# Order of the first loads, the root of block 0 and the grouping of LoRA products in a gated FFN kernel with an S4 convolution

## The chip, the cores and the metric

One core of a Trainium2 chip runs the kernel. The metric is the time of one execution on the device, in microseconds (us); the median of several runs counts. A profile is one execution recorded by the hardware; its times start with the span of that execution. PE is the matrix engine (PEld its weight loads), DVE the vector engine, ACT the scalar engine, POOL the GpSimd engine, SP the engine that issues most transfers.

## The reference, cut to what matters

The input x has 2 x 1024 tokens of 512 features, all in float32.

```python
xn = _layernorm(x, axis=-1)                       # mean and variance over the 512 features, eps 1e-5
s = _L0_attn_ref(xn, ...)                         # one S4 kernel K of 512 taps, causal convolution along the features, plus D*xn
def _lora_linear(x, w, a, b):                     # rank R = 16, SCALING = 2
    base = jnp.einsum('bsd,od->bso', x, w)
    low = jnp.einsum('bsr,or->bso', jnp.einsum('bsd,rd->bsr', x, a), b)
    return base + low * SCALING
h1 = _lora_linear(xn, w1, lora_A1, lora_B1)       # 512 -> 1376
h3 = _lora_linear(xn, w3, lora_A3, lora_B3)
g = _silu(_lora_linear(jax.nn.silu(h1) * h3, w2, lora_A2, lora_B2))   # 1376 -> 512
out = x + s * g
```

## The kernel before, in words

**Tiling.** The 2048 tokens are four blocks of 512 (`TB`), each of four tiles of 128 tokens (`NTT`). Two blocks form a super block (`sb`). A tile is normalized with tokens on the partitions, transposed on PE against an identity (L304) and copied by ACT out of PSUM (L312, L314, L315), so that features stand on the partitions. The 1376 hidden units are ten chunks of 128, taken in five pairs, and a last chunk of 96.

**Products by seven.** Each product of two 2x2 arrangements of blocks is made from seven block products instead of eight (Strassen's scheme in Winograd's form). For this DVE makes sums of token blocks (`outer_token_sum` L328, `inner_token_sum` L341 to L347) and of weight blocks (`outer_weight_sums` L441, `inner_weight_sum` L453), POOL those of the last chunk (L492 to L495). A `Chain` does the seven products on PE (L756), snapshots of PSUM on ACT (L776, L794), and totals on DVE (L780, L870). Pair 0 and the last chunk start with the outer scheme alone, since blocks 2 and 3 arrive later.

**LoRA** is merged into the weights: PE multiplies the two factors (`lora_product` L383, contraction over 16 rows) and DVE adds twice the result to the weights (`merge` L393). A set of factors lies at 32 * group of the partitions, 16 rows of it, and up to four groups can work at once in different row groups of PE. `lora_last` (L475) does the last chunk with groups 0 (w1) and 1 (w3); `merge_pair` (L408) does half of pair 0 with the same two groups, one half at a time; `merge_whole_pair` (L419) does a whole pair with four groups, whose groups 2 and 3 hold a second copy of the same factors.

**The opening.** `load_x` (L225) issues block 0's four tiles in turn on SP and ACT (L231). Then come the factors of groups 0 and 1, one set on SP and one on ACT (L372, L373), then on SP block 1 (four tiles), the last chunk's weights (L470), pair 0's weights (four transfers, L402), blocks 2 and 3, pair 1, and the second copy of the factors. Eight completion semaphores are used in turn, so that the ninth transfer and each one after it waits for the one eight places earlier. On ACT a one-element Silu (L973) brings the activation table in early. Keep-warm products of the identity (L991) fill PE at the start.

DVE makes mean and variance of each tile (`norm_stats`, L247 and L248) and the reciprocal root for the whole block (`norm_root`, L278: L281, then eight operations of `rsqrt` L57 to L66, then the shift L284). ACT and POOL normalize two tiles each (L293, L297).

**What sets the order.** The order on PE, DVE, ACT and POOL is the program's own: `manual_schedule` keeps what the program writes. In the opening (L965 to L1018) that is the written order; from there on an event list, `at(place, what)` and `after(delay, what)`, is popped by place (L1254). A place orders work and is no time: an instruction runs when its engine reaches it and its data are there. On PE the written order of the opening is: 18 keep-warm products, `lora_last` (8 products), 4 keep-warm products, the transposes of block 0, the first step of the last chunk, half of pair 0's LoRA (4 products), the next step, the transposes of block 1, the first step of pair 0, the other half of LoRA (4 products), and then products on token sums.

Of the kernel before, what the change touches and what calls it, by code (L numbers as in the profile page):

```python
# [12 lines left out]
F32 = mybir.dt.float32  # L13
# [4 lines left out]
P = 128  # L18
# [3 lines left out]
HID = 1376  # L22
# [27 lines left out]
def rsqrt(nc, pool, v, shape):  # L50


    y = pool.tile(shape, F32, tag="rs_y", name="rs_y")
    t = pool.tile(shape, F32, tag="rs_t", name="rs_t")
    part = 3.0 / 8.0
    c2 = part * 0.703952253
    nc.vector.tensor_scalar(  # L57
        y.bitcast(I32), v.bitcast(I32), -0.5, float(0x5F1FFFF9), ALU.mult, ALU.add
    )
    nc.vector.tensor_tensor(t, y, y, ALU.mult)  # L60
    nc.vector.scalar_tensor_tensor(t, t, -c2, v, ALU.mult, ALU.mult)
# [46 lines left out]
def s4_gated_ffn(  # L108
# [101 lines left out]
    def value(tag="s"):  # L210
        return upool.tile([P, TB], F32, tag=tag, name=tag, bufs={"s": 10, "c": 4}[tag])
# [11 lines left out]


    def load_x(b):  # L225
        room = (None, None, t_in[4], t_in[6])[b]
        tiles = []
        for tt in range(NTT):
            t = value() if room is None else room[:, tt, :]
            queue = nc.scalar if b == 0 and tt % 2 else nc.sync  # L230
            queue.dma_start(out=t, in_=x[bass.ds(b * TB + tt * P, P), :])  # L231
            tiles.append(t)
        return tiles

    norms, sums_of_x = {}, {}

# [38 lines left out]
            norms[b][:, :, 1], sums_of_x[b][:, 2, :], 1.0 / DIM, None, mult  # L275
        )

    def norm_root(mv, *blocks):  # L278
        n = len(blocks) * NTT
        veps = small.tile([P, n], F32, tag="veps", name="veps")  # L280
        nc.vector.tensor_scalar(veps, mv[:, :, 1], EPS, None, add)  # L281
        rstd = rsqrt(nc, small, veps, [P, n])
# [16 lines left out]
    def transpose(b, tiles, tag="aux"):  # L299
        sb, low = divmod(b, 2)  # L300
        for tt in tiles:
            ps = bank(tag)
            for dc in range(NDC):
                nc.tensor.transpose(  # L304
                    ps[:, dc * P : (dc + 1) * P],
                    x_in[b][tt][:, dc * P : (dc + 1) * P],
                    ident,
                )
            at_ = slice(tt * P, (tt + 1) * P)
            halves = ps.rearrange("p (c k t) -> p c k t", c=2, k=2)  # L310
            if low == 0:
                nc.scalar.copy(xr[:, 0:2, sb, :, at_], halves)  # L312
# [68 lines left out]
    def lora_product(ps, group, dc, lo, n, start=True):  # L381
        d, h = lora_factors(group, lo, n)
        nc.tensor.matmul(  # L383
            ps,
            lhsT=d[:, dc * P : (dc + 1) * P],
            rhs=h,
            start=start,
            stop=True,
            skip_group_check=True,
        )  # L390
# [14 lines left out]
                )  # L405
        return w

    def merge_pair(c, w, half, tag="aux"):  # L408

        ps = [bank(tag), bank(tag)]  # L410
        for k in range(2):
            for v in range(2):
                n = slice(k * 2 * P, (k + 1) * 2 * P)
                lora_product(ps[v][:, n], v, 2 * half + k, PAIR_AT[c], 2 * P, k == 0)
        for v in range(2):
            to = w[:, (1, 2, 0, 3)[2 * v + half]].rearrange("p k m h -> p (k m h)")
            after(1.6 + v, lambda to=to, v=v: merge(to, ps[v]))
# [45 lines left out]
    def load_last():  # L463
        both = const.tile([P, 2, 2 * NDC * LASTR], F32, tag="w2b", name="last")
        w, s = (
            both[:, i].rearrange("p (a b h) -> p a b h", a=n, h=LASTR)
            for i, n in enumerate((2, 4))
        )
        for v, src in enumerate((w1T, w3T)):
            nc.sync.dma_start(  # L470
                out=w[:, v], in_=src[:, LAST * P :].rearrange("(dc p) h -> p dc h", p=P)
            )
        return w, s

    def lora_last():  # L475
        ps = [bank("y"), bank("y")]
# [485 lines left out]
        for i, p in places:  # L962
            at(7 * n + p, lambda i=i: step(i))

    x_in = {0: load_x(0)}  # L965
    warm = const.tile([P, 1], F32, name="warm")
    nc.gpsimd.memset(warm, 0.0)
# [5 lines left out]
    nc.scalar.activation(warm, warm, AF.Silu)  # L973
    x_in[1] = load_x(1)
    make_upper_triangular(nc, tri, 1.0, diag=True)
    w_last, s_last = load_last()
    w_pair, s_pair = {0: load_pair(0)}, {c: {} for c in range(NPAIR)}
    x_in[2], x_in[3] = load_x(2), load_x(3)
    w_pair[1] = load_pair(1)
    for v, f in enumerate(factors):  # L980
        load_lora(nc.sync, 2 + v, *f, LSPLIT, HID)

    def other_factors():
        for v, (_, h) in enumerate(factors):
# [18 lines left out]
    ps_last = lora_last()  # L1003
    mv = norm_tile(0)
    norm_stats(0, range(NTT))
    norm_root(mv, 0)
    normalize(0)

    keep_warm(primed[1], 4)
    transpose(0, range(NTT))  # L1010
    mv = norm_tile(1)
    norm_stats(1, range(2))
    merge_last(w_last, ps_last, 0)
    norm_stats(1, range(2, NTT))
    norm_root(mv, 1)
    merge_last(w_last, ps_last, 1)
    mv_late = norm_tile(2, 3)
    ab_last = last_operands(w_last, s_last)  # L1018

# [37 lines left out]
            add_chain(2 + 7 * c + n, pair_chain(c, n), places)  # L1057
    at(-10, lambda: normalize(1))
    at(-9.9, lambda: last_sums(w_last, s_last))
    at(-9, lambda: merge_pair(0, w_pair[0], 0))  # L1060
    at(-3.8, lambda: merge_pair(0, w_pair[0], 1))
    for i in range(2):
        at(-6 + i, lambda i=i: transpose(1, range(2 * i, 2 * i + 2), "y"))
    for n, name in enumerate((3, 2, 1)):
        at((-2.3, -1.5, -0.45)[n], lambda name=name: outer_token_sum(0, name))
        at(-0.6 + 0.3 * n, lambda name=name: outer_weight_sums(w_pair[0], (name,)))
    at(0.4, lambda: outer_token_sum(0, 4))
    at(0.8, lambda: outer_weight_sums(w_pair[0], (4,)))
    for tt in range(NTT):
        at(-6 + 0.8 * tt, lambda tt=tt: norm_stats(2, (tt,)))  # L1070
        at(-1.4 + 0.1 * tt, lambda tt=tt: act_sums(3, tt))
        at((-0.3, -0.2, 1.7, 1.8)[tt], lambda tt=tt: act_squares(3, tt))
    at(-0.9, lambda: act_means(3))
    at(1.9, lambda: act_variances(3))
    at(6.9, lambda: norm_root(mv_late, 2, 3))
    at(7.3, lambda: normalize(2))
    at(7.7, lambda: normalize(3, (0,)))
    for n, place in enumerate((12.1, 12.8, 13.7, 14.4)):
        b, i = divmod(n, 2)
        at(place, lambda b=b, i=i: transpose(2 + b, range(2 * i, 2 * i + 2)))  # L1080
# [514 lines left out]
```

## Time and profile before

| what | value |
|---|---|
| runs | 442.51, 442.54, 442.62 us; median 442.54 |
| profiled execution | 442.84 us, of which the span is 441.0 us |
| busy in the span | PE 434.3 us (98%), DVE 317.6 (72%), POOL 207.9 (47%), ACT 144.3 (33%) |
| granted clock of PE | 0.998 of full speed, mean |
| transfers | 53.61 MB, mean 122 GB/s |
| first statistics on DVE | 3.98 us |
| `lora_last` on PE | from 7.89 us |
| first transposes of block 0 and of block 1 on PE | 11.01 and 18.11 us |
| first token sum (L328) on DVE | 21.55 us |

A row of the timeline is: start, length, engine, line, operation, written tile <- read tiles, shapes, count, and in brackets the idle time of that engine before it and what ended it. Rows of one kind that follow each other are put together, and a matmul in float32 is two records. A row of a table by stretch gives busy time (and count) of PE, PEld, DVE, ACT and POOL, then PE's granted clock, the share of the DMA engines that are busy, and GB/s. A row of a transfer gives the issuing queue, the count, the size and the median time from issue to landing.

### The profile page before, as it was taken

What the parts mean: (1) busy time and instruction counts of PE and PEld (TensorE: products, weight loads), DVE (VectorE), ACT (ScalarE), POOL (GpSimd) and SP (SyncE); (2) the same over time, 40 slices, a digit from 0 to 9 for tenths busy, and PEclk for the clock granted to TensorE, in tenths of its full rate; (3) what the DMA queues carried; (4) which work ended last, traced back from release to release, by engine and by line L of the source; (5) the groups of instructions that cost most, each with busy time, mean ns of one, the idle gap of its engine ahead of it and who ended that gap; (6) DMA issues with size and microseconds to landing.
All of it is one profiled execution on the core that took longest, in us unless ns stands there. A gap on an engine that the chain in (4) does not pass through costs nothing.

```text
span 441.0 us, 5158 instructions
## 1 busy us (share of the span) xinstructions
PE 434.3 (98%) x1704; PEld 269.1 (61%) x1704; DVE 317.6 (72%) x536; ACT 144.3 (33%) x296; POOL 207.9 (47%) x156
## 2 busy tenths in 40 slices
PE   7999999999999999999999999999999999999996
PEld 7645334344444444444443446888898999999996
DVE  5899999954974687469745796979786885653234
ACT  2777242453255324532453242211101212212221
POOL 1416468895689368946894468400000122222221
PEclk9999999999999999999999999999999999999999
DMA  8931304025102500250035526395901832422211
GB/s 242 364 83 44 124 0 149 10 84 159 36 24 80 159 24 25 88 170 25 25 129 206 162 94 214 94 364 189 344 33 71 296 129 95 144 97 95 77 67 48
DMA packets 35467, 53.61 MB, mean 122 GB/s; under 512 B 4689, under 2 KB 21521, under 8 KB 35313
## 3 DMA queue, kind: packets, MB, share of 16 engines
q1 hardware_dynamic: 35088, 52.69, 36.3%
q10 hardware_dynamic: 352, 0.60, 0.4%
q8 instruction: 13, 0.21, 0.2%
q14 instruction: 14, 0.11, 0.1%
HBM read 33.88 MB, written 19.40 MB: 121 GB/s over the span
## 4 chain that ended last, share of the span: by engine, by line
PE 86%; DVE 7%; DMA 2%; ACT 2%; issue 1%; POOL 0%; SPq 0%; DVEq 0%; ACTq 0%; POOLq 0%
PE x L756 43%; PE y L756 22%; PE w L756 11%; PE aux L930 4%; PE w L930 2%; DMA s<-in_x_dram 1%; DVE xt L328 1%; DVE s L453 1%; DVE w L441 1%; DMA w<-in_w1T_dram 1%; PE y L529 1%; PE aux L711 1%; DVE t_in L343 1%; ACT c L254 1%; DVE aux L1310 1%
## 5 line engine op out<-in xcount | busy, mean ns | idle before, releaser
L1313 POOL TENSOR_TENSOR o<-o,xin 128x512 f32<-128x512 f32 (+1 forms) x17 | 23.3, 1369 | 133.0 <-DVE o L1312 133.0
L837 POOL TENSOR_TENSOR s<-c,s 128x512 f32<-128x512 f32 (+1 forms) x44 | 63.2, 1442 | 17.6 <-ACT c L829 12.4
L776 ACT COPY s<-x 128x512 f32<-128x512 f32 (+1 forms) x54 | 31.5, 584 | 84.5 <-PE x L756 84.4
L756 PE MATMUL x<-t_in,s 128*128 128x512 f32 (+1 forms) x148 | 55.4, 501 | 0.0
L870 POOL TENSOR_TENSOR s<-ua_three,s 128x512 f32<-128x512 f32 x20 | 35.9, 1793 | 25.4 <-DVE s L780 25.4
L780 DVE TENSOR_TENSOR s<-s,y 128x512 f32<-128x512 f32 (+1 forms) x54 | 36.0, 679 | 15.7 <-PE y L756 10.6
L756 PEld LDWEIGHTS x<-t_in,s 128*128 128x128 f32 x148 | 26.6, 190 | 23.3 <-issue 11.7
L870 POOL TENSOR_TENSOR ua_three<-ua_three,s 128x512 f32<-128x512 f32 x20 | 30.6, 1529 | 13.8 <-DVE s L780 13.8
L756 PE MATMUL y<-t_in,s 128*128 128x256 f32 (+1 forms) x108 | 35.9, 459 | 0.1
L1335 ACT COPY z<-x 128x256 f32<-128x256 f32 x24 | 8.8, 371 | 70.5 <-PE x L756 70.4
L870 POOL TENSOR_TENSOR s<-u_three,s 128x512 f32<-128x512 f32 x20 | 29.4, 1474 | 1.8 <-ACT c L829 1.0
L1310 DVE TENSOR_TENSOR aux<-aux,m 128x384 f32<-128x384 f32 x32 | 18.1, 565 | 15.8 <-PE aux L930 14.3
L829 ACT ACTIVATE c<-c 128x512 f32<-128x512 f32 x40 | 25.2, 632 | 12.9 <-DVE c L870 12.9
L756 PEld LDWEIGHTS y<-t_in,s 128*128 128x128 f32 x108 | 20.1, 190 | 11.6 <-issue 8.1
L794 ACT COPY w<-x 128x512 f32<-128x512 f32 (+1 forms) x37 | 21.1, 570 | 11.6 <-PE x L756 11.5
L870 POOL TENSOR_TENSOR u_three<-ua_three,u_three 128x512 f32<-128x512 f32 x10 | 15.6, 1556 | 13.4 <-DVE u_three L780 13.3
L756 PE MATMUL x<-t_in,w 128*128 128x512 f32 x40 | 21.0, 605 | 0.0
L756 PE MATMUL x<-xt,w 128*128 128x512 f32 x40 | 20.7, 598 | 0.0
L756 PE MATMUL x<-xr,w 128*128 128x512 f32 x40 | 20.6, 614 | 0.0
L756 PE MATMUL x<-xr,s 128*128 128x512 f32 x40 | 20.5, 614 | 0.0
L756 PE MATMUL x<-xt,s 128*128 128x512 f32 x40 | 20.4, 592 | 0.0
L756 PE MATMUL y<-xt,w 128*128 128x512 f32 x40 | 19.8, 592 | 0.0
(302 smaller groups left out, 908.7 us busy)
## 6 DMA issues: line engine op xcount, KB each, us to landing
g_dram<-s SPq DMA_DIRECT2D x40, 256.0 KB, 2.1
g<-g_dram SPq DMA_DIRECT2D x10, 512.0 KB, 5.8
xin<-in_x_dram SPq DMA_DIRECT2D x16, 256.0 KB, 2.7
out_dram<-o SPq DMA_DIRECT2D x14, 256.0 KB, 2.0
t_in<-g_dram SPq DMA_DIRECT2D x6, 512.0 KB, 4.1
w<-in_w1T_dram SPq DMA_DIRECT2D x10, 256.0 KB, 3.6
w<-in_w3T_dram SPq DMA_DIRECT2D x10, 256.0 KB, 4.9
t_in<-in_x_dram SPq DMA_DIRECT2D x8, 256.0 KB, 5.7
```

Of the source, the lines that this page charges most:

```text
L254: nc.scalar.activation(value("c"), x_in[b][tt], AF.Copy, accum_out=sums_of_x[b][:, 0, tt : tt + 1])
L756: nc.tensor.matmul(ps[:, cols], lhsT=lhsT, rhs=rhs if parts == 1 else rhs[:, cols], start=first and i == 0 and part == 0, stop=i == len(pa ...
L776: nc.scalar.copy(t, self.x)
L780: nc.vector.tensor_tensor(t, t, self.y, add)
L794: nc.scalar.copy(self.w, self.x)
L829: nc.scalar.activation(c, c if src is None else src, AF.Silu)
L837: nc.gpsimd.tensor_tensor(g, act, g, mult)
L870: (nc.vector if o < 20 else nc.gpsimd).tensor_tensor(to, a, b, add)
L930: nc.tensor.matmul(to[:, n * P : (n + 1) * P], lhsT=x_, rhs=by, start=start, stop=True, skip_group_check=True,)
L1310: nc.vector.tensor_tensor(y[:, P:], y[:, P:], m[:, n * P : (n + 3) * P], add)
L1313: (nc.vector if last else nc.gpsimd).tensor_tensor(o, o, self.xin[h][:, cols], add)
L1335: nc.scalar.copy(t, xb)
```

## The change

Four things change together.

- **Loads.** Block 1 is two transfers of 512 KB, one on SP and one on ACT, issued right behind block 0's tiles and into the room of `t_in[7]`. The factors of groups 0 and 1 follow, then on SP the last chunk's weights, the second copy of the factors (groups 2 and 3, formerly last), pair 0, blocks 2 and 3 (two transfers each instead of four), pair 1.
- **Root.** Block 0's root is a Sqrt on ACT, a reciprocal on DVE and one Newton step on DVE. The early table load is that of Sqrt; a one-element Silu behind the copies of block 0's transposes brings the other table in. The other blocks keep `rsqrt`.
- **LoRA of pair 0** is done by `merge_whole_pair` with four groups in one pass, ahead of block 1's transposes; `merge_pair` is gone. On DVE its four merges follow each other behind block 1's root.
- **Places.** Three keep-warm products instead of four ahead of block 0's transposes, whose third tile uses a bank of tag x; block 1's first tile borrows a bank of x; merging of the last chunk's w3 goes ahead of block 1's root; three of block 2's four tiles of statistics go from between the merges and the first token sums to behind the weight sums (places -5.2, -4.4, -3.6 to 0.84, 0.85, 0.9); normalization of block 2 goes from 7.3 to 7.7.

On ACT the silu of the last chunk (`c<-w`, L829) now comes behind all copies of block 1 instead of between them.

```diff
     def load_x(b):
...
+        if b == 0:
+            tiles = [value() for _ in range(NTT)]
+            for tt, t in enumerate(tiles):
+                (nc.sync, nc.scalar)[tt % 2].dma_start(out=t, in_=x[bass.ds(tt * P, P), :])
+            return tiles
+        room = (None, t_in[7], t_in[4], t_in[6])[b]
+        for tt in range(0, NTT, 2):
+            queue = nc.scalar if b == 1 and tt else nc.sync
+            queue.dma_start(
+                out=room[:, tt : tt + 2, :],
+                in_=x[bass.ds(b * TB + tt * P, 2 * P), :].rearrange("(n p) d -> p n d", p=P),
+            )
+        return [room[:, tt, :] for tt in range(NTT)]
...
+    def refined(mv, veps):
+
+        shape = list(veps.shape)
+        y = small.tile(shape, F32, tag="rs_y", name="rs_y")
+        t = small.tile(shape, F32, tag="rs_t", name="rs_t")
+        root = small.tile(shape, F32, tag="root", name="root", bufs=1)
+        nc.scalar.activation(root, mv[:, :, 1], AF.Sqrt, bias=eps)
+        nc.vector.tensor_scalar(veps, mv[:, :, 1], EPS, None, add)
+        nc.vector.reciprocal(y, root)
+        nc.vector.tensor_tensor(t, y, y, mult)
+        nc.vector.scalar_tensor_tensor(t, t, -0.5, veps, mult, mult)
+        nc.vector.scalar_tensor_tensor(y, t, 1.5, y, add, mult)
+        return y
...
-    x_in = {0: load_x(0)}
+    x_in = {0: load_x(0), 1: load_x(1)}
...
-    nc.scalar.activation(warm, warm, AF.Silu)
-    x_in[1] = load_x(1)
+    nc.scalar.activation(warm, warm, AF.Sqrt)
+    w_last, s_last, load_of_last = load_last()
+    for v in range(2):
+        load_of_last(v)
     make_upper_triangular(nc, tri, 1.0, diag=True)
-    w_last, s_last = load_last()
+    for v, f in enumerate(factors):
+        load_lora(nc.sync, 2 + v, *f, LSPLIT, HID)
     w_pair, s_pair = {0: load_pair(0)}, {c: {} for c in range(NPAIR)}
     x_in[2], x_in[3] = load_x(2), load_x(3)
     w_pair[1] = load_pair(1)
-    for v, f in enumerate(factors):
-        load_lora(nc.sync, 2 + v, *f, LSPLIT, HID)
...
-    norm_root(mv, 0)
+    norm_root(mv, 0, on_act=True)
     normalize(0)
 
-    keep_warm(primed[1], 4)
-    transpose(0, range(NTT))
+    keep_warm(primed[1], 3)
+    for tt, tag in enumerate(("aux", "aux", "x", "aux")):
+        transpose(0, (tt,), tag)
+    nc.scalar.activation(warm, warm, AF.Silu)
     mv = norm_tile(1)
     norm_stats(1, range(2))
     merge_last(w_last, ps_last, 0)
     norm_stats(1, range(2, NTT))
+    merge_last(w_last, ps_last, 1)
     norm_root(mv, 1)
-    merge_last(w_last, ps_last, 1)
...
-    at(-9, lambda: merge_pair(0, w_pair[0], 0))
-    at(-3.8, lambda: merge_pair(0, w_pair[0], 1))
-    for i in range(2):
-        at(-6 + i, lambda i=i: transpose(1, range(2 * i, 2 * i + 2), "y"))
+    at(
+        -9,
+        lambda: merge_whole_pair(
+            0, w_pair[0], [bank("y"), bank("y")], (1.6, 1.7, 1.8, 1.9)
+        ),
+    )
+    at(-6, lambda: transpose(1, (0,), "x", True))
+    at(-5.9, lambda: transpose(1, range(1, NTT), "y"))
...
-        at(-6 + 0.8 * tt, lambda tt=tt: norm_stats(2, (tt,)))
+        at((-6, 0.84, 0.85, 0.9)[tt], lambda tt=tt: norm_stats(2, (tt,)))
...
-    at(7.3, lambda: normalize(2))
-    at(7.7, lambda: normalize(3, (0,)))
+    at(7.7, lambda: normalize(2))
+    at(7.75, lambda: normalize(3, (0,)))
```

More of the change, by code (lines that the diff above doesn't have):

```diff
@@ L225, in load_x @@
     def load_x(b):
[L226 to L233, printed above, removed]
+        if b == 0:
[11 more added lines that the diff above has]
+        return [room[:, tt, :] for tt in range(NTT)]
     norms, sums_of_x = {}, {}
@@ L276, in act_variances, with norm_root @@
         )
-    def norm_root(mv, *blocks):
+    def refined(mv, veps):
[10 more added lines that the diff above has]
+        return y
+    def norm_root(mv, *blocks, on_act=False):
         n = len(blocks) * NTT
         veps = small.tile([P, n], F32, tag="veps", name="veps")
-        nc.vector.tensor_scalar(veps, mv[:, :, 1], EPS, None, add)
-        rstd = rsqrt(nc, small, veps, [P, n])
+        if on_act:
+            rstd = refined(mv, veps)
+        else:
+            nc.vector.tensor_scalar(veps, mv[:, :, 1], EPS, None, add)
+            rstd = rsqrt(nc, small, veps, [P, n])
         shift = small.tile([P, n], F32, tag="shift", name="shift")
@@ L297, in normalize, with transpose @@
                 nc.gpsimd.tensor_scalar(t, t, rstd[:, one], shift[:, one], mult, add)
-    def transpose(b, tiles, tag="aux"):
+    def transpose(b, tiles, tag="aux", borrow=False):
         sb, low = divmod(b, 2)
         for tt in tiles:
-            ps = bank(tag)
+            ps = bank(tag, borrow)
             for dc in range(NDC):
@@ L406, in load_pair @@
         return w
[L408 to L417, printed above, removed]
     def merge_whole_pair(c, w, first=None, delays=(1.15, 2.3, 4.3, 4.4)):
@@ L468, in load_last, with load @@
         )
-        for v, src in enumerate((w1T, w3T)):
+        def load(v):
             nc.sync.dma_start(
-                out=w[:, v], in_=src[:, LAST * P :].rearrange("(dc p) h -> p dc h", p=P)
+                out=w[:, v],
+                in_=(w1T, w3T)[v][:, LAST * P :].rearrange("(dc p) h -> p dc h", p=P),
             )
-        return w, s
+        return w, s, load
     def lora_last():
@@ L963, in add_chain @@
             at(7 * n + p, lambda i=i: step(i))
-    x_in = {0: load_x(0)}
+    x_in = {0: load_x(0), 1: load_x(1)}
     warm = const.tile([P, 1], F32, name="warm")
-    nc.gpsimd.memset(warm, 0.0)
+    eps = const.tile([P, 1], F32, name="eps")
+    for t, v in ((warm, 0.0), (eps, EPS)):
+        nc.gpsimd.memset(t, v)
     make_identity(nc, ident)
```

## The prediction

> **What bounds the kernel now.** I read the page first (PE is 98% busy, so only PE's first microseconds and its tail hold idle time), then the busy times by stretch:
>
> ```profile
> core 0: us, PE busy (x) PEld busy (x) DVE busy (x) ACT busy (x) POOL busy (x), PEclk, DMA share, GB/s
> 4.00:12.00 8.00, 7.11 (x58) 6.53 (x57) 6.70 (x23) 1.89 (x4) 1.52 (x2) 1.00 1.00 272
> 12.00:22.00 10.00, 9.46 (x51) 5.76 (x52) 8.64 (x27) 7.11 (x17) 3.77 (x6) 1.00 1.06 371
> 22.00:56.00 34.00, 34.00 (x120) 15.19 (x116) 33.17 (x53) 19.20 (x45) 13.96 (x11) 1.00 0.27 82
> 56.00:83.00 27.00, 26.93 (x62) 10.92 (x62) 26.97 (x27) 9.41 (x17) 21.50 (x11) 1.00 0.19 61
> 83.00:120.00 37.00, 36.89 (x98) 15.12 (x97) 26.21 (x36) 15.13 (x27) 29.15 (x20) 1.00 0.27 86
> ```
>
> From 22 to 83 us two engines are full at once: PE 60.9 of 61 us, DVE 60.1 of 61. Only after 83 us does DVE get air (26 of 37). So what the opening does reaches the end only if both engines come out of it earlier, and the later of the two decides. That DVE has no slack is seen where PE waits for it at 56 us:
>
> ```profile
> 55.35 0.67 DVE L870 TENSOR_TENSOR c<-ua_one,x 128x512 f32<-128x512 f32 x1
> 55.95 2.28 DVE L341 TENSOR_TENSOR t_in<-xt 128x2048 f32<-128x2048 f32 x1
> 56.08 0.30 PEld L756 LDWEIGHTS x<-t_in,s 128*128 128x128 f32 x2 [0.79 <-DVE c L870]
> ```
>
> The sum on DVE ends at 56.02 and PE's next product into that bank starts at 56.08, behind a short stall. Any later DVE here is a later end. Third, the opening on PE:
>
> ```profile
> 7.89 1.28 PE L383 MATMUL y<-lo_h,lo_d 16*128 16x96 f32 x16
> 9.10 1.16 PE L991 MATMUL w<-ident 128*128 128x128 f32 x8
> 11.01 1.09 PE L304 MATMUL aux<-ident,s 128*128 128x128 f32 x8 [0.75 <-ACT s L293]
> 12.34 1.21 PE L304 MATMUL aux<-ident,s 128*128 128x128 f32 x8 [0.24 <-ACT xr L312]
> 13.38 1.94 PE L756 MATMUL x<-xr,last 128*96 128x256 f32 x8
> 15.26 1.13 PE L383 MATMUL aux<-lo_h,lo_d 16*128 16x256 f32 x8
> 16.32 1.96 PE L756 MATMUL w<-xr,last 128*96 128x512 f32 x4
> 18.11 1.04 PE L304 MATMUL y<-ident,s 128*128 128x128 f32 x8
> ```
>
> PE works in program order: LoRA of the last chunk (needs all four factor loads), keep-warm products, block 0's transposes, and so on. The transposes wait 0.75 us for block 0's normalized tile; the factors are there at 7.87. Last, the transfers of the first 12 us, in slices of 0.3 us:
>
> ```profile
> GB/s 0 0 0 0 0 48 137 232 389 410 389 410 389 430 362 377 247 173 97 137 179 131 89 157 300 396 389 382 396 382 340 262 208 280 271 289 274 277 280 297
> lo_h<-in_b1T_dram SPq DMA_DIRECT2D x1, 38.0 KB, 5.7
> lo_h<-in_b3T_dram ACTq DMA_DIRECT2D x1, 38.0 KB, 5.8
> ```
>
> Block 0 (1.05 MB) flows at about 390 GB/s until 4.8 us. The four factor transfers (140 KB) follow, and from 4.8 to 7.2 us the rate falls to 151 GB/s. They land 5.7 to 5.8 us after an issue at 2.1, which is 7.8 to 7.9.
>
> **The change, part by part.** Times are of the profiled execution (span 441.0, execution 442.84); the median shown is 442.54, so I add the difference that I find to 442.54.
>
> *Transfers.* Block 1's two 512 KB transfers now stand on both queues ahead of the factors, and the instruction order shows the first factor load of each queue behind them and the second behind a wait for block 0's first tiles as well. Good: block 0's third tile was late,
>
> ```profile
> 6.43 0.69 DVE L247 BATCH_NORM_STATS2 stats<-s 128x6 f32<-128x512 f32 x1 [0.74 <-DMA s<-in_x_dram]
> ```
>
> in the stretch in which the factors move. Without them there DVE loses the 0.74 and a little more; statistics of block 0 end at 7.30 instead of 8.13. Bad: the factors stand behind 1.05 MB more. At 390 GB/s that is 2.69 us: 7.87 + 2.69 = 10.56. Against it, 363 KB passed between 4.8 and 7.2, of which 223 KB were block 1's first tiles; without these the factors could be 223/390 = 0.57 us quicker, 10.0. I take 10.3 (both ends kept; a bound from far below is 7.9, if the factors are not held by block 1 at all).
>
> *Root.* Nine small operations at 0.2 us pitch (8.17 to 10.11) become one Sqrt on ACT and five operations on DVE. The nearest rows for the Sqrt are 0.20 us (the 128x1 ACTIVATE of L973) and 0.81 (128x512 of L293); 128x4 is nearest to the first. The reciprocal of 128x4 at L669 took 0.178. So 0.2 + 5 x 0.2 = 1.2 with the handoffs, 0.7 saved: normalization starts at about 8.6 instead of 10.14 and block 0's first tile is ready at 9.4. That is **worth nothing if PE is not there**: what hides it is the LoRA of the last chunk, which stands ahead of the transposes on PE. From 10.3: 1.23 us for it (7.87 to 9.10), 0.76 for six records of keep-warm, so the transposes start at 12.3, **1.3 later than 11.01**. This is the step that I think decides.
>
> *From there to block 1's transposes.* Before 18.11 - 11.01 = 7.10. The third tile goes to another bank, so the wait of 0.24 goes: 6.86. LoRA with four groups is 8 products instead of 4 in that place, but the pass at 30.48, which has four groups already, took 1.07 for 16 records, and the two-group pass 1.06 for 8. So nothing is added here: 19.17, 1.06 later than before.
>
> *What else the queue is moved past.* SP issues the second factor set (about 8 to 10 us, needed on PE at 16.4) ahead of pair 0's weights, so these are issued at about 10.4 instead of 8.46 and land near 16 (before, the last row of issue is 10.14 and DVE used them at 16.42 and 22.76). All four are now wanted by the four merges at 17.4: 1.4 us to spare, hidden behind PE's late opening; with an early opening it would be gone. Block 2's normalization goes behind three statistics, its transposes on PE are at 36.90 and the tiles are normalized from 32.2 on: some 3 us to spare, nothing.
>
> *ACT.* A table load enters between the copies of block 0 (end 15.25) and the copy w<-x of L794. The load took 1.28 and the warm ACTIVATE 0.20:
>
> ```profile
> 2.58 1.28 ACT L973 ACT_TABLE_LOAD   x1 [2.58 <-issue]
> 3.88 0.20 ACT L973 ACTIVATE warm<-warm 128x1 f32<-128x1 f32 x1
> ```
>
> So w<-x runs from 16.75 to 17.3; PE wants it at 17.37, after the LoRA pass. Hidden, by 0.05. Normalization of block 1 waits behind it: its ACT tiles end at 18.1 and 18.9, before the transposes at 19.17 want them. No row shows a load among work: one end is the row, the other twice the row, 1.2 us more on the path. I take the row, the only one of its kind. At the start, the first load stands behind a factor issue that waits for a tile of block 0 (4.1): it ends at about 6, still ahead of the Sqrt.
>
> [...]
>
> *From block 1's transposes to the token sums.* Before, 18.11 to 21.55 (first xt on DVE) = 3.44. The silu c<-w stood among ACT's copies (19.81 to 20.30) and is now behind them: 2.95. The first sum starts at 22.12, **0.57 later**. DVE is free before that: LoRA's four merges follow PE's pass at 17.4 and end near 19.9, one tile of statistics near 20.7.
>
> *DVE from the token sums on.* Two merges leave this stretch (0.60 each by pitch, 22.76 to 23.36), three tiles of block 2's statistics enter it (0.80 each by pitch, 17.63 to 20.03 for three): -1.2 + 2.4 = +1.2. Idle time that can take it up between 21.55 and 55.35: 0.11 at 30.06 and 0.23 at 34.0. So L870 at 55.35 comes 0.57 + 1.2 - 0.34 = **1.43 late**. PE alone would be late by only 0.26 there, since the second LoRA pass (21.47 to 22.53, 1.06) is gone from its queue and its first product on token sums goes from 22.53 to 22.8. DVE decides: **+1.43**, 442.54 + 1.43 = **444.0**. Nothing behind 83 us gives it back, PE being full to 400 us. In short: difference = landing of the factors - 8.87.
>
> **Rivals.**
> 1. *The factors are not late (faster).* If the sixteen rows of a factor pass beside block 1 and land by 7.9, block 0's transposes start at 9.9, and every later step follows: 7.9 - 8.87 = -1.0, **441.5**. It decides from 8.87 down. For it: the factors are only 140 KB, and they landed at 7.9 beside block 1's first tiles. Against: those tiles were requested after them (3.97, 4.36), and each queue serves 1.05 MB for both in the order requested as far as the landings show.
> 2. *DVE's extra is absorbed (no change that can be measured).* If the statistics fall into time that DVE idles before the sums, or the factors land near 9.4, PE's +0.26 is what is left: **442.8**. For it: DVE idles about 1.4 us before the sums. Against: the order on DVE is fixed, and three tiles stand behind the sums.
> 3. *The table switch costs twice its row:* +1.43 + 1.2, **445.2**. Against: ACT ran 0.02 us behind the first load.
> That the root does nothing for the end is part of the forecast, not a rival.
>
> **How the numbers follow.** Forecast 0.51 (its own range 443.4 to 444.6: factors at 10.0 to 10.6, with 0.25 more on each side for how they straggle); rival 1 0.17; rival 2 0.20; rival 3 0.12. This kernel's measurement can tell about 0.2% (0.89 us) from no change. Faster by more: 0.17. Within: rival 2 and the forecast's lower edge, 0.25. Slower: 0.58. The range leaves out most of rival 1 and what lies above rival 3: 442.0 to 445.4.
>
> **What would show it.** In the changed profile: statistics of block 0 without a wait (third tile near 5.6); the shift ready near 8.5; LoRA of the last chunk on PE near 10.3 and the transposes near 12.3, PE idle before them for the factors; block 1's transposes near 19.2; the first xt near 22.1; the L870 at 55.35 near 56.8 and PE idle there by about 1 us. Wrong, if LoRA of the last chunk runs before 8.9 us, if PE shows no wait for DVE between 50 and 62 us, or if ACT shows idle time beside the second table load.

## The result and the profile after

The changed kernel takes **447.79 us** (median; 446.84 to 448.84), the kernel before beside it 442.52 (441.86 to 442.62): ratio 1.0125, 95% interval 1.0111 to 1.0138. That is 5.3 us more, where 1.4 were forecast; the time lies above the forecast range of 442.0 to 445.4. The profiled execution is the longest of them, 448.84 with a span of 447.1 (before 442.84 and 441.0), so its steps add up to +6.0.

The table by stretch of the changed kernel, with the columns of the one of before (PE, PEld, DVE, ACT, POOL, then granted clock, DMA share, GB/s):

```profile
4.00:12.00 8.00, 3.56 (x27) 3.37 (x26) 5.05 (x17) 3.30 (x5) 1.52 (x2) 1.00 0.94 240
12.00:22.00 10.00, 10.00 (x63) 8.67 (x64) 4.86 (x19) 4.59 (x8) 3.44 (x6) 0.66 0.88 274
22.00:56.00 34.00, 32.59 (x123) 15.63 (x124) 31.69 (x58) 23.03 (x56) 11.77 (x12) 1.00 0.35 120
56.00:83.00 27.00, 26.56 (x61) 10.44 (x60) 26.88 (x25) 7.40 (x14) 20.97 (x9) 1.00 0.20 61
```

The first two rows are the news. From 4 to 12 us PE works 3.56 us instead of 7.11: it idles. In the next stretch it is "full", but at a granted clock of 0.66: it is busy and slow, which a column of busy times alone would hide. Cut at the clock's own edges, the table has 0.50 throughout 12.07 to 18.90. The opening on PE says what the idling waits for:

```profile
11.94 2.25 PE L405 MATMUL y<-lo_h,lo_d 16*128 16x96 f32 x16 [4.44 <-DMA lo_h<-in_b1T_dram]
14.12 1.65 PE L1008 MATMUL w<-ident 128*128 128x128 f32 x6
15.56 1.92 PE L326 MATMUL aux<-ident,s 128*128 128x128 f32 x8
...
23.68 0.60 PE L326 MATMUL x<-ident,t_in 128*128 128x128 f32 x4
```

The factors come at 11.94, not 10.3, and PE has done nothing for 4.44 us by then. The same LoRA pass (L383 before, now L405) then lasts 2.25 us where it lasted 1.28, and two tiles of transposes 1.92 instead of 1.09. DVE and the place where PE waits for it:

```profile
11.07 0.69 DVE L252 BATCH_NORM_STATS2 stats<-t_in 128x6 f32<-128x512 f32 x1 [2.36 <-DMA t_in<-in_x_dram]
...
26.97 1.29 DVE L350 TENSOR_TENSOR xt<-xr,b 128x512 f32<-128x512 f32 x2 [1.69 <-ACT xr L337]
...
61.61 0.67 DVE L884 TENSOR_TENSOR c<-ua_one,x 128x512 f32<-128x512 f32 x1
62.33 1.13 PE L770 MATMUL x<-t_in,s 128*128 128x512 f32 x2 [0.37 <-DVE c L884]
```

The sum that stood at 55.35 stands at 61.61 (+6.26), and PE still waits for it. Of this, +5.42 is there at the first token sum already (21.55 to 26.97). Block 1's first tile, requested ahead of the factors now, is read at 11.07 after an idle of 2.36 us. Last, the rates of the first 12 us, 0.3 us a slice:

```profile
GB/s 0 0 0 0 0 48 61 164 328 423 403 389 417 410 396 403 342 280 382 355 287 362 375 369 423 360 294 152 103 135 141 131 132 204 234 125 59 25 20 19
```

The bulk, 2.1 MB of both blocks, is through at about 8.1 us; then the rate falls to between 103 and 234 GB/s, and from 10.8 below 60, with the factors still not complete.

### The profile page after: what moved, and what is told of

Its sections match the earlier page's. It is cut to its first block, busy times and chain, and to the rows that moved or that the text cites. A ratio compares the mean times of both kernels' runs of the same rounds, so it can differ in the third digit from the quotient of the medians.

```text
span 447.1 us, 5155 instructions
## 1 busy us (share of the span) xinstructions
PE 435.6 (97%) x1702; PEld 271.2 (61%) x1702; DVE 316.4 (71%) x532; ACT 146.2 (33%) x299; POOL 209.7 (47%) x157
## 4 chain that ended last, share of the span: by engine, by line
PE 84%; DVE 3%; ACT 0%; issue 0%; DVEq 0%; ACTq 0%
PE x L770 42%; PE y L770 22%; PE w L770 11%; PE aux L944 4%; PE w L944 2%; PE y L405 1%; PE y L543 1%; PE aux L725 1%; DVE t_in L365 1%; DVE aux L1333 0%; DVE xt L350 0%; DVE o L1335 0%; DVE t_in L363 0%; PE aux L655 0%; ACT o L1293 0%; ACT c L843 0%
## 5 line engine op out<-in xcount | busy, mean ns | idle before, releaser
L794 DVE TENSOR_TENSOR s<-s,y 128x512 f32<-128x512 f32 (+1 forms) x54 | 35.9, 678 | 15.6 <-PE y L770 10.6
```

The costliest lines, as they stand in the source:

```text
L794: nc.vector.tensor_tensor(t, t, self.y, add)
```

## The experiments

**Theory.** The order of the loads is the loss: the factors land late, PE stands still for them, and its clock falls for what follows. **Rivals:** the other parts of the change (DVE's statistics behind the sums, the second factor set, the table switch) cost a good part of it.

### Undoing the order, and doing it alone

`a_factors_first` is the changed kernel with one line moved:

```diff
-    x_in = {0: load_x(0), 1: load_x(1)}
+    x_in = {0: load_x(0)}
...
         load_lora((nc.sync, nc.scalar)[v], v, *f, LSPLIT, HID)
+    x_in[1] = load_x(1)
```

> The changed kernel with one thing put back: the factors of groups 0 and 1 are requested behind block 0 and ahead of block 1, as before. Theory A (the late factors are the whole loss: PE waits 4.4 us for them, and its granted clock then falls to half for 6.8 us): factors on PE by 8.0 us, clock full throughout, block 0's transposes at 10.4, and the time falls to or below that of before, 441.5 to 442.5. Rival B (the table switch on ACT and three tiles of statistics behind the token sums cost most of the 5 us): 446 or more, whatever the factors do.

Measured: 443.32 (442.12 to 446.14, ten executions), ratio 1.0018 (0.9996 to 1.0041). LoRA on PE is at 7.80, the transposes are at 10.32, the first token sum on DVE at 20.56:

```profile
7.80 1.28 PE L405 MATMUL y<-lo_h,lo_d 16*128 16x96 f32 x16 [0.36 <-DMA lo_h<-in_b1T_dram]
```

```profile
20.56 1.29 DVE L350 TENSOR_TENSOR xt<-xr,b 128x512 f32<-128x512 f32 x2 [1.30 <-ACT xr L337]
```

So 4.5 of the 5.3 us go with the order. The median is 0.8 above what theory A expected at most, and the interval leaves open whether anything of the loss stays. The wide spread is taken up below.

`b_block1_first` is the kernel before with block 1's two transfers (written as in the changed kernel) ahead of the factors, and nothing else.

```diff
-    x_in = {0: load_x(0)}
+    x_in = {0: load_x(0), 1: load_x(1)}
...
-    x_in[1] = load_x(1)
```

> The kernel before with one thing changed: block 1 in two transfers ahead of the factors of groups 0 and 1; root, LoRA grouping and places stay. Theory A: factors near 11.9 us, PE idle some 4 us ahead of them, half clock after it, time 447 to 448. Rival B: 443 or less, since neither the table switch nor the statistics have moved.

Measured: 447.77 (447.54 to 449.62), ratio 1.0126 (1.0101 to 1.0152). LoRA is at 11.04 behind 3.62 us of idling, block 0's transposes are 3.77 us long from 14.51 (before: 2.54 from 11.01), and the mean clock is 0.992:

```profile
11.04 1.67 PE L391 MATMUL y<-lo_h,lo_d 16*128 16x96 f32 x16 [3.62 <-DMA lo_h<-in_b1T_dram]
12.64 2.08 PE L998 MATMUL w<-ident 128*128 128x128 f32 x8
14.51 3.77 PE L312 MATMUL aux<-ident,s 128*128 128x128 f32 x16
```

The order alone costs 5.15 us, about as much as the four parts together (5.27).

`b_root` is the kernel before with block 0's root on ACT and the Silu behind block 0's copies, and nothing else.

```diff
-    norm_root(mv, 0)
+    norm_root(mv, 0, on_act=True)
...
     transpose(0, range(NTT))
+    nc.scalar.activation(warm, warm, AF.Silu)
```

> The kernel before with block 0's root alone changed (Sqrt on ACT, Newton step, the table switch behind block 0's copies); loads, LoRA grouping and places stay. From the rows: root 0.7 us shorter, block 0's transposes 10.4 instead of 11.0, both PE and DVE earlier by 0.6: 441.9. Rival B, or a table switch that holds the copy w<-x up: 443 or more.

Measured: 442.43 (441.55 to 443.15, ten executions), ratio 0.9997 (0.9986 to 1.0009). The normalization is earlier and PE's transposes with it, 10.28 instead of 11.01, but the time shows no difference (441.9 was expected). Neither the root nor the second table load is behind the loss.

### The clock

`a_more_warm` is the changed kernel with 22 more products of the identity ahead of the last chunk's LoRA, which are to fill PE until the factors are there. They are not needed for the result of the computation, like the other keep-warm products.

```diff
         keep_warm(ps, 9, True)
+    keep_warm(primed[1], 22)
```

> The changed kernel with 22 more keep-warm products on PE ahead of the last chunk's LoRA, so that PE is busy until the factors land; loads as in the change. Theory A with the clock as a separate term: factors still near 11.9, but the clock stays full, which saves 1.0 us on that LoRA, 0.7 on the keep-warm products and 1.3 on the transposes of block 0, together 2.9 us: 444.9. If the lower clock costs nothing on the path (the block's landing bounds instead): 447.8 as the change.

Measured: 446.22 (445.41 to 446.84), ratio 1.0081 (1.0061 to 1.0102), mean clock 0.998 to 1.0 instead of 0.991 to 0.996. Its opening on PE, with the first token sum on DVE:

```profile
12.36 1.13 PE L405 MATMUL y<-lo_h,lo_d 16*128 16x96 f32 x16
13.43 0.94 PE L1008 MATMUL w<-ident 128*128 128x128 f32 x6
14.20 1.04 PE L326 MATMUL aux<-ident,s 128*128 128x128 f32 x8
...
20.84 0.60 PE L326 MATMUL x<-ident,t_in 128*128 128x128 f32 x4
```

```profile
24.12 1.29 DVE L350 TENSOR_TENSOR xt<-xr,b 128x512 f32<-128x512 f32 x2 [1.69 <-ACT xr L337]
```

The clock is 1.00 throughout. The added products run till 12.43, longer than needed: the two factor loads that come last have landed at 11.41 and 11.60 here. So the factors are used 0.42 us later than in the changed kernel, and still block 1's transposes start 2.84 earlier and the first sum 2.85 earlier: the slow clock was worth some 3 us of the profiled execution. Of the medians, the products give back 1.6 (444.9 was expected, 446.22 measured); the four executions of the changed kernel differ in it (0.996 in those of 446.84 and 447.57, 0.991 in those of 448.01 and 448.84).

In the changed kernel the clock was 0.50 for 6.83 us (12.07 to 18.90) behind an idle time of 4.44, with a mean of 0.991; in its executions with a mean of 0.996 it was some 3.6 us of half clock by an estimate (0.004 of some 445 us, lost at half speed). The other profiles show 6.83 us of half clock behind 3.62 and 4.05 us of idling (`b_block1_first`, `a_means_act`), 3.41 behind 3.41 and 3.61 (`a_last_later` and `a_spread`, both below), and none behind 1.36 (`a_lora_behind`, below). What decides between these lengths, no run shows.

### Why the factors needed till 11.9

`a_last_later`: in the changed kernel the last chunk's weights (384 KB in rows of 384 bytes) are requested at 5.26 and pass beside the factors. Here they wait for a small POOL write behind block 0's normalization, and the requests behind them on SP (second factor set, pair 0, blocks 2 and 3, pair 1) move along in the program.

```diff
     normalize(0)
+    for v in range(2):
+        nc.gpsimd.memset(w_last[:, v, 0, 0:1], 0.0)
+    for v in range(2):
+        load_of_last(v)
```

> The changed kernel, but the last chunk's weights (384 KB in rows of 384 bytes) are requested only behind the normalization of block 0, near 10.2 us, instead of at 5.26 and 5.69. In the changed kernel their pieces pass between 8 and 11 us, beside the factors. Theory A (the factors share the DMA engines with these weights): the factors land about as long behind block 1 as they did behind block 0 before, 8.1 + 2.4 = 10.5, and LoRA of the last chunk starts on PE at 10.3 to 10.8. Rival B (the factor rows take 3.8 us by themselves): LoRA stays near 11.9. In both the last chunk's weights come later (about 12.5), which its merges, near 14 to 15, still survive; by A the time is 446 to 447, by B 447.5 to 448.5.

Measured: 447.51 (446.65 to 448.18), ratio 1.0109 (1.0091 to 1.0127). PE and the rates:

```profile
11.15 1.30 PE L405 MATMUL y<-lo_h,lo_d 16*128 16x96 f32 x16 [3.41 <-DMA lo_h<-in_b1T_dram]
```

```profile
GB/s 0 0 0 0 0 41 55 137 389 355 410 396 410 396 403 396 301 355 341 321 355 416 410 376 410 371 329 129 44 47 45 14 22 15 23 0 0 34 75 130
```

LoRA at 11.15 lies between the two expectations. Without the weights, and with hardly any other traffic (14 to 47 GB/s from 8.4 to 10.5 us), the factors still take until 11.15, 3.05 us behind the bulk. Two loads of the second factor set were issued at 5.31 and 5.67, in the weights' place, so that the factors are not alone here either. The time moves by 0.3 us, within its spread. Nor do the 0.79 us against 11.94 show a price of the weights: the factor load that PE waits for landed at 11.90, 11.50, 11.41 and 11.22 in four profiles with the loads of the changed kernel (itself, `a_means_act`, `a_more_warm`, `a_lora_behind`), at 11.10 here, and at 11.00 in `b_block1_first`, which has the weights beside it.

The landings of the single parts of a transfer show what is waited for. Each transfer of the opening lands in sixteen parts. In the changed kernel, fifteen parts of block 1's first transfer have landed by 8.46 us and the sixteenth at 11.04; of its second, fifteen by 9.85 and the last at 11.44; of one factor load, fifteen by 9.16 and the last at 11.24. In the kernel before, block 0's third tile had fifteen by 5.61 and the last at 6.40. In this execution of the changed kernel one part in sixteen holds back all eight transfers from block 1 to the last chunk's weights, by 1.3 to 2.6 us, those requested ahead of the factors included. Other executions differ: in `a_means_act` two parts are late (block 1's first transfer: fourteen by 8.81, then 10.00 and 10.25). What waits for a transfer waits for its last part here: in the changed kernel DVE reads block 1's first tile at 11.07, behind the part of 11.04, and PE begins LoRA at 11.94, behind a last part of 11.90.

`a_spread` moves one of the two factor sets to other partitions:

```diff
-    lora = {}
+    lora, ROWS_AT = {}, (0, 64, 32, 96)
...
-        rows = slice(32 * group, 32 * group + R)
+        rows = slice(ROWS_AT[group], ROWS_AT[group] + R)
```

> The changed kernel, but groups 1 and 2 exchange their rows: the first two factor sets lie on partitions 0 to 15 and 64 to 79 instead of 0 to 15 and 32 to 47. Without the last chunk's weights beside them the factors still needed 3.05 us behind block 1 (8.1 to 11.15), with their last rows of 2432 bytes passing one after the other at 98 ns. Theory (the two sets get in each other's way where they are written): the factors land 1 to 1.5 us earlier, LoRA of the last chunk on PE at 10.4 to 10.9, block 1's first tile before 10, time 444.5 to 446.5. Rival (it is the rows themselves, wherever they go): LoRA at 11.5 to 12, 447 to 448.5. [...]

Measured: 447.48 (445.70 to 447.82), ratio 1.0093 (1.0072 to 1.0113). LoRA at 11.59 and block 1's first tile at 10.73: the rival. Block 1's first transfer now has fifteen parts by 9.23 and the last at 10.70. Between 8.15 and 9.3 us, pieces of 2432 bytes take 268 to 389 ns in `a_last_later` and 98 to 222 here. That fits two sets that get in each other's way, but doesn't show it: with the sets unmoved, the four such pieces of `a_more_warm` take 118 to 219. From 8.6 to 10.6 us pieces of 2048 and 2432 bytes still start about one every 0.1 us and take 0.1 us each. LoRA moved by 0.35, not by 1 to 1.5, and the landing, 11.55, lies among the four of the unchanged loads (11.22 to 11.90). The 1 to 1.5 us were the author's assumption that the two sets get in each other's way where they are written; no run shows it. What the late parts wait for, the traces don't tell: this stays open.

`a_lora_behind` puts the last chunk's LoRA behind block 0's transposes in PE's order.

```diff
-    ps_last = lora_last()
...
         transpose(0, (tt,), tag)
+    ps_last = lora_last()
```

> The changed kernel, but LoRA of the last chunk stands behind block 0's transposes on PE instead of ahead of them. If the order on PE carries the lateness (PE waits for the factors while block 0 is ready): transposes near 9.6, PE idle for about 2.2 us instead of 4.4, LoRA near 12 to 12.5, the last chunk's first product near 15.3 behind its merge, block 1's transposes near 20.5, first token sum on DVE near 23.5, time 444.5 to 445.5. Rival: the landing of the factors alone sets the end, so that the order is worth nothing: 447.5 to 448.

Measured: 445.88 (444.90 to 447.46), ratio 1.0085 (1.0062 to 1.0108). The transposes start at 9.62, the first token sum at 21.78, only 0.23 behind the kernel before. The factors land nearly as late as in the changed kernel (11.22 and 11.44, used at 11.61), but PE idles for 1.36 us only and the clock stays at 1.00 from 4 to 120 us of the profile (0.999 in the mean; 0.992 to 1.0 in the four executions). So it is PE's program order that passes on nearly the whole lateness of the factors, and in the profiled executions the slow clock with it. Still the time is 3.4 above before, and above the 444.5 to 445.5 that were expected: its trace has another wait, as follows. No run takes that wait out of this version.

### A small POOL operation that is held up

`a_ff_stats1` is `a_factors_first` with one of the three moved tiles of statistics back at its place ahead of the sums:

```diff
-        at((-6, 0.84, 0.85, 0.9)[tt], lambda tt=tt: norm_stats(2, (tt,)))
+        at((-6, -5.2, 0.85, 0.9)[tt], lambda tt=tt: norm_stats(2, (tt,)))
```

> The changed kernel with the factors requested ahead of block 1 again, and one of the three moved tiles of block 2's statistics put back ahead of the token sums, where DVE idled 1.30 us. Theory (DVE's work behind the sums decides): the first sum still starts near 20.6, the sum that PE waits for near 54.4 instead of 55.21, and the time is about 0.6 below the same kernel without this (PE had 0.63 idle in 22 to 56 us): ratio to the kernel before 0.997 to 0.999. Rival (statistics are absorbed, DVE is not the bound): no difference to the version without it.

Measured: 444.72, but in two heaps: 441.38 to 441.86 (three of twelve executions) and 443.58 to 445.24 (nine, of which five have a mean clock of 0.998 or more). Ratio 1.0032 (1.0012 to 1.0052). `b_lora4` is the kernel before with nothing but the four-group pass, the second factor set behind the last chunk's weights and the banks of block 1's transposes as in the changed kernel:

```diff
-    at(-9, lambda: merge_pair(0, w_pair[0], 0))
-    at(-3.8, lambda: merge_pair(0, w_pair[0], 1))
+    at(-9, lambda: merge_whole_pair(0, w_pair[0], [bank("y"), bank("y")], (1.6, 1.7, 1.8, 1.9)))
```

> The kernel before with nothing but LoRA of pair 0 four groups at a time: second copy of the factors requested behind the last chunk's weights, one pass ahead of block 1's transposes, block 2's statistics left where they were. Theory (the part is worth what the rows say): PE loses the second pass of 1.06 us behind block 1's transposes, DVE's two late merges (1.2) go ahead of the token sums; the first sum starts within 0.5 us of 21.55, the sum on DVE at 55.35 comes 0.7 to 1.2 earlier, time 441.5 to 442.0. Rival (four more loads of 16 rows delay pair 0's weights and so the merges): first sum 1 us or more later, time 442.5 to 443.5.

Measured: 446.44 (446.09 to 447.27), ratio 1.0089 (1.0071 to 1.0106), worse than either expectation. The profile of `a_ff_stats1` shows what both share; first POOL, then PE, then DVE:

```profile
24.97 2.82 POOL L265 TENSOR_SCALAR act_sums<-act_sums 128x4 f32<-128x4 f32 x1 [5.17 <-ACT c L259]
```

```profile
29.95 1.93 PE L770 MATMUL x<-xt,last 128*96 128x512 f32 x4 [2.51 <-ACT s L790]
```

```profile
23.40 1.29 DVE L350 TENSOR_TENSOR xt<-b,xr 128x512 f32<-128x512 f32 x2
24.61 1.29 DVE L452 TENSOR_TENSOR w<-w 128x512 f32<-128x512 f32 x2
25.81 1.29 DVE L350 TENSOR_TENSOR xt<-xr,xt 128x512 f32<-128x512 f32 x2
27.01 0.69 DVE L452 TENSOR_TENSOR w<-w 128x512 f32<-128x512 f32 x1
27.61 0.69 DVE L252 BATCH_NORM_STATS2 stats<-t_in 128x6 f32<-128x512 f32 x1
```

An operation on 4 elements a partition lasts 2.82 us on POOL: from 24.97 to 27.79, just behind the last of DVE's row of TENSOR_TENSORs (27.01 to 27.70). ACT waits for its result, its copy out of PSUM stands behind that, and PE stands 2.51 us. In `b_lora4` it is 4.10 us and in `a_lora_behind` 3.77, with the same 2.5 us on PE. In the kernel before the operation meets a merge on DVE:

```profile
24.56 0.68 DVE L393 SCALAR_TENSOR_TENSOR w<-aux,w 128x512 f32<-128x512 f32 x1
24.71 0.22 POOL L260 TENSOR_SCALAR act_sums<-act_sums 128x4 f32<-128x4 f32 x1 [4.98 <-ACT c L254]
```

It takes 0.22 us there. The change moved these merges ahead of the sums, so that the operation meets an unbroken row of TENSOR_TENSORs. That row alone does not make it long: in the profile of the changed kernel it took 0.28,

```profile
30.47 0.28 POOL L265 TENSOR_SCALAR act_sums<-act_sums 128x4 f32<-128x4 f32 x1 [8.16 <-ACT c L259]
```

and it was as short in four other profiles (0.27 or 0.28 in `a_factors_first`, `a_more_warm`, `a_last_later`, `a_spread`). In all five the operation started 0.11 or 0.12 us ahead of DVE's next instruction; in the three where it was held up, 0.24, 0.31 and 0.59 ahead. Such a late start goes with the short duration; no run varies it alone.

Where it was held up, the operation stayed over some five to seven DVE instructions in a row (2.82, 3.77 and 4.10 us) and ended 0.09 us behind the last TENSOR_TENSOR of that row (which ends at 27.70, 29.09 and 29.43). So it seems to wait for the end of the row; why, the traces don't tell.

Four kernels test what this costs, with block 3's means on ACT instead of POOL (two operations of 0.2 us):

```diff
-        nc.gpsimd.tensor_scalar(sums[:, 1, :], sums[:, 0, :], -1.0 / DIM, None, mult)
-        nc.gpsimd.tensor_scalar(norms[b][:, :, 0], sums[:, 0, :], 1.0 / DIM, None, mult)
+        nc.scalar.activation(sums[:, 1, :], sums[:, 0, :], AF.Copy, scale=-1.0 / DIM)
+        nc.scalar.activation(norms[b][:, :, 0], sums[:, 0, :], AF.Copy, scale=1.0 / DIM)
```

> The changed kernel, but the two small operations that turn block 3's sums into means (128x4 each) run on ACT instead of POOL. In the traces of three other versions the first of them took 2.82, 3.77 and 4.10 us on POOL instead of 0.22, beside an unbroken row of TENSOR_TENSORs on DVE, ACT waited for it and PE 2.50 us for ACT. In the profiled execution of the changed kernel it took 0.28, so theory: the loss of this change does not come from it, 447.0 to 448.0 as before. Rival: it strikes in most of the executions that are not profiled, and the time falls to 444.5 to 446.

> The changed kernel with the factors requested ahead of block 1 again, and block 3's means on ACT instead of POOL. Theory (the spread of 442.1 to 446.1 us without the second edit comes from the POOL operation that is held up in some executions): all executions lie within 441.9 to 442.7. Rival (the spread comes from the transfers): it remains, 442.1 to 446.

> The version before this one and one tile of block 2's statistics put back ahead of the token sums. Theory: DVE's work behind the sums decides once POOL is out of the way, so the time is 0.6 below the version without this edit, 441.3 to 441.9 in all executions; ratio to the kernel before 0.997 to 0.999. Rival: PE is the bound there and nothing changes between the two versions, 441.9 to 442.7.

> The kernel before with LoRA of pair 0 four groups at a time and block 3's means on ACT. Theory (the 4 us that the four-group pass cost alone are the held-up POOL operation, 3.1 to 3.3 us at the sum on DVE, and little else): 442.0 to 443.0, PE without the wait of 2.51 us for ACT. Rival (the second factor set's transfers cost the time): 445.5 to 446.5, as without the edit.

| kernel | POOL | means on ACT |
|---|---|---|
| changed | 447.79 (446.84 to 448.84) | `a_means_act` 448.66 (446.79 to 450.08), ratio 1.0127 (1.0096 to 1.0157) |
| factors first | 443.32 (442.12 to 446.14) | `a_ff_means` 443.29 (442.71 to 443.94), ratio 1.0009 (0.9996 to 1.0022) |
| the same, one tile of statistics back | 444.72 (441.38 to 445.24) | `a_ff_stats1_means` 442.29 (441.66 to 443.15), ratio 0.9988 (0.9973 to 1.0002) |
| before, four-group LoRA alone | 446.44 (446.09 to 447.27) | `b_lora4_means` 443.43 (442.95 to 447.12), ratio 1.0024 (1.0003 to 1.0045) |

The upper heap of `a_ff_stats1` is gone and the waits of 2.5 us with it; the edit is worth 2.4 to 3.0 us where the operation was held up. (Two of the ten executions of `b_lora4_means`, 446.23 and 447.12, have a lower mean clock, 0.996 and 0.991.) In the changed kernel it is worth nothing, so its loss is not that: the theory holds there. From `a_factors_first` to `a_ff_means` the spread falls from 4.0 to 1.2 us, while the median stays; of the long executions of `a_factors_first`, 446.14 and 444.45 also have a lower mean clock, 0.992 and 0.996. `a_ff_means`, `a_ff_stats1_means` and `b_lora4_means` came out 0.4 to 0.6 above what was expected of them; `b_lora4_means` waits 0.73 us for a merge on DVE at 106.82, which the kernel before doesn't. One tile of statistics ahead of the sums is worth 1.0 us (443.29 to 442.29; DVE's sum at 54.31 instead of 55.53): DVE is the bound that it was taken for.

```profile
55.53 0.67 DVE L884 TENSOR_TENSOR c<-ua_one,x 128x512 f32<-128x512 f32 x1
```

```profile
54.31 0.67 DVE L884 TENSOR_TENSOR c<-ua_one,x 128x512 f32<-128x512 f32 x1
```

### Versions that might beat both

The moved factor set together with factors first. `a_ff_stats1_spread` is `a_ff_stats1_means` with it, `b_root_spread` is `b_root` with it.

> The changed kernel with the factors requested first again, one tile of block 2's statistics back ahead of the token sums, block 3's means on ACT, and the first two factor sets on partitions 0 to 15 and 64 to 79. Theory: factors on PE near 6.8 to 7.3 instead of 7.6, which is worth little as block 0's transposes wait for the normalized tile near 10.1; block 1's transfers come earlier: 441.8 to 442.3, ratio to the kernel before 0.998 to 0.9995. Rival: no difference to the version without it, 442.3.

Measured: 442.15 (441.42 to 443.37), ratio 0.9981 (0.9971 to 0.9992); factors used at 7.14. The version without the moved set has 0.9988 (0.9973 to 1.0002), so no difference between the two is shown.

> The kernel before with nothing but block 0's root on ACT and the first two factor sets on partitions 0 to 15 and 64 to 79. Theory: block 0's third tile waits less (0.74 us before), normalization starts earlier by some 0.5 us and PE's transposes with it: 441.5 to 442.0, ratio 0.997 to 0.999. Rival: the sets' rows hold the tile up as before, 442.4.

Measured: **441.47** (441.15 to 442.83), ratio 0.9964 (0.9951 to 0.9977): below both kernels, and 1.6 (0.4%) below the kernel before beside it (443.05). The intervals of `b_root` and of this version do not overlap, so the moved set seems to be worth some 0.3% here. In its profile, of the slowest of the six executions, statistics of block 0 run almost without a wait (third tile 5.75; 6.11 in `b_root`, 6.43 before), and the shift is ready at 8.68. Whether that wait makes the difference is not shown: `a_ff_stats1_means` reads the third tile at 5.72 without the move.

## Why the prediction was wrong

The direction and the deciding step (factors behind block 1, then all of PE behind them) were right; two sizes failed: the factors' landing, and the price of PE's idling. Against the profiled execution:

- **"From 10.3 ... the transposes start at 12.3": 11.94 and 15.56.** This step failed twice. The landing was worked out as what it was before, plus bytes over the bulk rate, 2.69 us, less 0.26 for block 1's tiles that no longer pass beside the factors. The bulk took from 4.8 to 8.1 us (3.3, at some 320 GB/s): 0.6 more. The 0.26 were not gained. And the tail behind the bulk, until the last part is there, was 3.07 before (4.8 to 7.87) and 3.84 in this execution: 0.77 more. In `a_last_later` the tail is 3.05, and four profiles with the loads of the changed kernel differ by 0.7 among themselves, so what makes the tail longer here stays open.
- **What was left out: PE's clock.** The prediction says "PE idle before them for the factors" and gives that idling no price beyond its length. Behind the 4.44 us of it the clock was 0.50 for 6.83 us: 3.62 us instead of 2.0 from LoRA to the transposes, 8.12 instead of 6.86 from there to block 1's transposes, 2.9 together. With PE kept busy (`a_more_warm`) the same steps take 1.84 and 6.64, and the short formula, fed with the start of LoRA in place of the landing, gives 12.36 - 8.87 = +3.5 against +3.2 measured in span. The formula held at full clock; it was fed a start 1.6 too early and lacked the clock.
- **"2.95" from block 1's transposes to the first sum:** 3.29, 0.34 short.
- **"DVE decides", +0.86 between first sum and L870:** 33.80 before, 34.64 after, +0.84. Right, and PE waits there, 0.37 us (about 1 was said).
- Together 1.64 of landing, 2.88 of clock, 0.34, less 0.02: 4.84, which is 61.61 less the 56.78 that the prediction puts there.
- **Statistics, root, normalization:** third tile 5.65, shift 8.55, normalization 8.74, and worth nothing. Right.
- **The table load "hidden, by 0.05":** it ran 19.75 to 21.03, and w<-x behind it ended before PE had left the LoRA pass:

```profile
19.75 1.28 ACT L1029 ACT_TABLE_LOAD   x1
21.04 0.20 ACT L1029 ACTIVATE warm<-warm 128x1 f32<-128x1 f32 x1
21.15 0.58 ACT L808 COPY w<-x 96x512 f32<-96x512 f32 x1
```

  PE's product behind that pass started at 21.89 without a wait. Rival 3 fails: the ACTIVATE follows 0.01 us behind the load's 1.28.
- **Rival 1** (factors pass beside block 1) fails by the landing. **Rival 2** (DVE's extra is absorbed) fails: `a_ff_stats1_means` against `a_ff_means` shows it at 1.0.
- **"Second factor set, pair 0": nothing.** Right for the changed kernel, where DVE waits for PE and not for pair 0 at the merges (21.98). But "LoRA four at a time" was costed for its products and merges alone. That with two merges moved a 128x4 operation on POOL can last 2.82 to 4.10 us instead of 0.22 was not seen; in the changed kernel it cost nothing, as the operation took 0.28 in its profile; by itself the pass costs 3 us (`b_lora4` less `b_lora4_means`).

## What to carry to other kernels

Ahead of moving a small transfer behind a large one, look at the landing of its last part, not at bytes over rate (11.90 instead of 10.3 here), and price the idle time that it makes on PE twice: once for its length (4.44 us here), and once for the clock behind it (0.50 for 6.83 us, worth 2.9). Cheap products that keep PE busy until the data are there (22 in `a_more_warm`) brought block 1's transposes 2.84 us forward here. A move that looks neutral on two engines can still lengthen an operation of one of them (0.27 us on POOL in `a_factors_first`, 2.82 in `a_ff_stats1`): look for a small operation whose duration differs between profiles.

## What had not been expected of the hardware

- PE's clock fell to 0.50 for 6.83 us behind 4.44 us of idling (0.996 to 0.991 in the mean over an execution, 3 us at the first token sum of the profiled one), and for 3.41 or 6.83 behind 3.41 to 4.05 in other versions.
- Beside loads of 16 rows, one of the sixteen parts of each of eight transfers landed 1.3 to 2.6 us behind the other fifteen in the profiled execution of the changed kernel (8.46 and 11.04 for block 1's first). Why is open.
- The first of the two 128x4 operations of block 3's means took 0.22 to 0.28 us or 2.82 to 4.10 on POOL; beside DVE's unbroken row of TENSOR_TENSORs both were seen (0.28 in the changed kernel, 2.82 in `a_ff_stats1`).
